# Convolutional attention on one core: first image's query norms taken with chunk-wise products, and 36 convolution taps of its second row group moved to TensorE

## The chip, the cores and the metric

The kernel runs on one core of one Trainium2 chip. The metric is the device time of one execution in microseconds (us). Before the change the median of three runs is 2868.29 us (2864.83 to 2871.43). The execution that was profiled took 2862.87 us, of which the trace spans 2861.1 us; the remaining 1.8 us lie outside the program's first and last instruction.

## What is computed

The input is four images of 384 channels and 48 x 48 points, in 32-bit floats. The reference, cut to what matters here:

```
local = depthwise 7x7 convolution of x, scaled and shifted per channel
x_norm = layernorm(x over channels)
q, k, v = split(x_norm @ qkv_w.T + qkv_b), 8 heads of 48
q = q + layernorm(local over channels)
attn = softmax(q @ k.T / sqrt(48)); out = attn @ v
out = x + (out @ proj_w.T + proj_b)
```

So every query needs the convolution of its point and a layernorm of it over the 384 channels ("the query norm"), on top of the usual projection.

## The kernel before

Channels lie on the partitions, in three chunks of 128. An image's 2304 points are cut into six groups of 8 image rows, 384 points each; there are 24 groups in all, counted by `t`. Keys and values of a whole image are made first (`from_x`, L574), then the six query groups are run one after the other. A group's attention is 12 slots (`for s in range(NSLOT)`, L1111): four pairs of heads, and three batches of six key blocks for each. A slot has two halves. In the first, TensorE (PE) makes the scores (`score_batch`, L888) and ScalarE (ACT) exponentiates them (L896); in the second, PE weighs the values (`weigh_batch`, L903).

The convolution runs beside that on VectorE (DVE), as one multiply-add for each of 49 taps and three chunks (L288, or L284 for a first tap): 147 operations for a group. All groups' operations stand in one stream, in order (`conv_ops`, L263; `stream`, L929). `convolve(point)` takes the number of operations that `plan` (L362) has given to a half slot. The plan knows for each half slot a spare DVE time (`spare`, L315) and for each group a due point: `due` (L359) asks that the 147 operations of group t are through before half 0 of slot `norm_slots(t - 1)[0]` of the group before. That slot is 8 in group 0 and 5 in all later ones (L313). The plan takes at each half slot the fastest rate that any of the next twelve due points asks for, so an early due point makes all that comes before it denser.

When a group's convolution is done, its query norm follows (class `Norm`, L384), spread over slots:

- For group 1, worked on in group 0 (slots 7 to 11): DVE adds the three chunks (`sum`, L408 and L409), PE multiplies the sum by a matrix of 1/384 (`mean_kept`, L429) to have the mean on every partition, ACT copies it to SBUF (L431), DVE subtracts it (`centre`, L440), ACT squares (L403), and the same sum and product of the squares give the variance. ACT takes its root (`root`, L447 to L449), DVE refines it (`newton`, L454 and L455).
- For all other groups: DVE adds the chunks, transposes in blocks of 32 and reduces (L464, L465), two DMAs on SP's queue write the partial sums to DRAM and read them back spread over the partitions (`out`, L468 and L469), and DVE reduces those (`few_in`, L478), transposes back (L485, L505) and goes on. That happens twice for a norm, for the mean and for the variance; the root is taken of 12 numbers a partition (L497 to L499).

Then `local_end` (L738) scales the convolution, `query_end` (L747) adds it to the projected query, `high_queries` (L760) and `low_queries` (L765, with the `qs<-qs` DMAs of L770 and L772 on SP) split the query of a head pair in two parts and place them for the scores, and `gather_tails` (L521) collects the fourth pair.

The order of the instructions on PE, DVE and ACT is the order of the program's text (L84); each of them works through its own list in order. SP's and POOL's lists are ordered by the framework. PSUM is four buffers of two banks, taken in turn by everything on PE.

At the start of the kernel (L948 to L1037) keys, values and projected queries of the first image are made, with the norms of x on PE and the convolution of group 0 and the first 10 operations of group 1 on DVE (`convolve_first`). Ten taps of chunk 0 of group 0 are done on PE as products with a diagonal matrix of the tap's 128 weights (`first_products`, L298). ACT makes those matrices (L296). The stage ends with `query_end(0)`, `high_queries(0, 0)`, `low_queries(0, 0)` (L1031 to L1033), and the scores of group 0 begin.

Of the kernel before, what the change touches and what calls it, by code (L numbers as in the profile page):

```python
# [16 lines left out]
P = 128  # L17
# [11 lines left out]
OUT_SLOT = 4  # L29
WARM = 14  # L30
PE_TAPS = 10

# [13 lines left out]
def unshifted_pass(  # L46
# [39 lines left out]
    def two_banks(name="r"):  # L86
        return ps.tile([P, 2, 512], F32, tag="r", name=name)
# [175 lines left out]
    def conv_ops(t):  # L263
        b, g = divmod(t, NG)
        if t + 1 < NT:
            load_slab(*divmod(t + 1, NG))
        slab, first, end = slabs[b, g]
        acc = work.tile([P, CC, G], F32, tag="acc", name=f"acc{t}", bufs=3)
        accs[t] = acc
        if t == 0:  # L270
            nc.vector.memset(acc[:, 0, :], 0.0)

        order = [(tap, c) for tap in taps for c in range(CC)]
        if t == 0:
            mine = [(tap, 0) for tap in taps[PE_TAPS:]]
            order = [o for o in order if o[1]] + mine
        for tap, c in order:
            part = window(slab, acc[:, c, :], g, first, end, c, tap)
            if not part:
                continue  # L280
            src, dst = part
            weight = cw[:, c, tap : tap + 1]
            if tap == taps[0]:
                nc.vector.tensor_scalar(  # L284
                    dst, src, weight, shift[:, c : c + 1], ALU.mult, ALU.add
                )
            else:
                nc.vector.scalar_tensor_tensor(dst, src, weight, dst, ALU.mult, ALU.add)  # L288
# [9 lines left out]
    def first_products():  # L298
        first_sum = two_banks()[:, 0, :G]
        slab, first, end = slabs[0, 0]  # L300
        for i, tap in enumerate(taps[:PE_TAPS]):
            src, part = window(slab, first_sum, 0, first, end, 0, tap)
            nc.tensor.matmul(
                part, lhsT=diagonal(i), rhs=src, start=i == 0, stop=i == PE_TAPS - 1
            )
        return first_sum
# [77 lines left out]
    class Norm:  # L384
# [38 lines left out]
            self.m = two_banks()[:, 0, :G] if m is None else m  # L423
            project(self.m, lambda c: mean_w, lambda c: src[:, c, :])

        def mean_kept(self):

            m = two_banks()[:, 0, :G]
            nc.tensor.matmul(m, lhsT=mean_w, rhs=self.buf[:, 0, :], start=True, stop=True)  # L429
            self.m = self.buf[:, 0, :]  # L430
            nc.scalar.copy(self.m, m)  # L431

# [540 lines left out]
    next(making)  # L973
    for c in range(CC):
        scale_rows(0, c)
    first_sum = first_products()
    m, bank = columns()
    convolve_first(10)
    norm = Norm(xn[0, 1])
# [15 lines left out]
    norm.scale(norm.newton())  # L995
    both(making)
    convolve_first(7)
    for g in range(1, NG):

        last = g == NG - 1  # L1000
        making = from_x(0, g)
        both(making)
        assert not last or n_first >= each - PE_TAPS
        norm = Norm(accs[0] if last else xn[0, g + 1])
        norm.mean_by_chunk(norm.src)
        if last:
# [24 lines left out]
    query_end(0)  # L1031
    high_queries(0, 0)
    low_queries(0, 0)  # L1033
# [5 lines left out]
    for t in range(NT):  # L1039
        b, g = divmod(t, NG)  # L1040
        if g == 0 and b:
# [4 lines left out]
            for gk in range(NG):  # L1046
# [57 lines left out]
                both(making)  # L1104
                if gk < NG - 2:
                    ao = fetch(before + 1)
        following = g < NG - 1
        next_image = b + 1 < B
        coming = next_image and g >= later(b + 1)
        first, second = norm_slots(t)  # L1110
        for s in range(NSLOT):  # L1111
            pair, third = divmod(s, KB // BATCH)
            if third == 1 and pair < NP - 1:
                high_queries(t, pair + 1)
            score_batch(t, s)
            if pair < NP - 1 or g < NG - 1:
                load_keys(b, (pair + 1) % NP, third)
# [17 lines left out]
            if coming and s == X_SLOTS[1] + 1:  # L1135
                norm_x.scale(norm_x.few_newton())
            if following and s == second + 1:
                local_end(t + 1, norm.few_newton() if t else norm.newton())
# [8 lines left out]
            if t and following and s == second:  # L1147
                norm.few_variance()
            convolve("slot", t, s, 0)
            sums_add()  # L1150
            if t == 0 and s in (first, second):
                norm.mean_kept()
            if coming and s == X_SLOTS[1]:
                norm_x.few_root()
            if following and s == second:
                norm.few_root() if t else norm.root()
            if s == first and t == 0:
                norm.centre()
# [9 lines left out]
            if t and following and s == first:  # L1168
                norm.few_centre()
            if s == OUT_SLOT and g:  # L1170
                ao = outputs[t - 1][0]
# [9 lines left out]
            if following and s == first - 1:  # L1181
                norm = Norm(accs[t + 1])
                norm.sum()
                if t:
                    norm.out()
            if following and s == first + 1:
                norm.sum_squares()
                if t:
                    norm.out()

    sums_add()
    for before in range(NT - NG, NT):
# [556 lines left out]
```

## Time and profile before

| what | value |
|---|---|
| median of three runs | 2868.29 us |
| profiled execution | 2862.87 us, span 2861.1 us |
| PE, DVE, ACT busy | 2771.2, 2458.6, 1635.9 us |
| start to the first score of group 0 | 164.4 us |
| group 0, 1, 2, 3, 4, 5 (first score to first score) | 116.1, 101.8, 104.8, 104.0, 101.0, 88.4 us |
| keys and values of image 1 | 139.9 us |
| groups 6 to 10 (image 1) | 90.4, 88.3, 91.6, 98.2, 90.1 us |

A group's time is the distance between the first score product of its slot 0 and that of the next group; it is read off the timeline. A slot without a wait takes 7.36 us, so a group takes at least 12 x 7.36 = 88.3 us. The profile's windows view gives for each stretch of time the busy microseconds of every engine and the number of its instructions, and then the granted share of TensorE's clock. A product of 32-bit floats shows as two matmul records.

### The profile page before, as it was taken

What the parts mean: (1) busy time and instruction counts of PE and PEld (TensorE: products, weight loads), DVE (VectorE), ACT (ScalarE), POOL (GpSimd) and SP (SyncE); (2) the same over time, 40 slices, a digit from 0 to 9 for tenths busy, and PEclk for the clock granted to TensorE, in tenths of its full rate; (3) what the DMA queues carried; (4) which work ended last, traced back from release to release, by engine and by line L of the source; (5) the groups of instructions that cost most, each with busy time, mean ns of one, the idle gap of its engine ahead of it and who ended that gap; (6) DMA issues with size and microseconds to landing.
All of it is one profiled execution on the core that took longest, in us unless ns stands there. A gap on an engine that the chain in (4) does not pass through costs nothing.

```text
span 2861.1 us, 53602 instructions
## 1 busy us (share of the span) xinstructions
PE 2771.2 (97%) x19238; PEld 1742.0 (61%) x19238; DVE 2458.6 (86%) x4875; ACT 1635.9 (57%) x2632; POOL 592.4 (21%) x1125
## 2 busy tenths in 40 slices
PE   9987989899999999999999999999999999999999
PEld 6654555565655666656665666666665566666665
DVE  7789898899889999988989999989988999999502
ACT  4345656566622766666642466766662266676662
POOL 5720000000067001000026401000005610011000
PEclk9998999999999999999999999999999999999999
DMA  7444444544555555446445554554554555445541
GB/s 140 107 138 113 130 123 133 149 127 129 145 153 136 170 155 164 126 136 179 150 112 155 167 148 148 170 154 128 150 157 136 140 169 159 139 136 179 168 160 62
DMA packets 197461, 410.57 MB, mean 144 GB/s; under 512 B 69888, under 2 KB 140480, under 8 KB 196672
## 3 DMA queue, kind: packets, MB, share of 16 engines
q0 software_dynamic: 65440, 254.88, 26.9%
q1 hardware_dynamic: 128752, 148.55, 21.2%
q8 instruction: 154, 2.52, 0.4%
q10 hardware_dynamic: 2992, 3.62, 0.4%
q14 instruction: 123, 1.01, 0.1%
HBM read 298.44 MB, written 64.78 MB: 127 GB/s over the span
## 4 chain that ended last, share of the span: by engine, by line
PE 69%; DVE 18%; DMA 8%; POOL 2%; issue 1%; ACT 1%; SPq 1%; DVEq 0%; ACTq 0%; POOLq 0%
PE o L903 30%; PE r L888 26%; PE r L515 13%; DVE acc L288 13%; DMA parts<-part 2%; DMA four<-parts 2%; DMA wide<-k 1%; DMA qs<-qs 1%; DMA slab<-in_x_dram 1%; POOL wide L540 0%; DVE ao L807 0%; DVE sq L409 0%; DVE qs L765 0%; DMA start_up<-in_qkv_wT_dram 0%; DVE k L603 0%
## 5 line engine op out<-in xcount | busy, mean ns | idle before, releaser
L288 DVE SCALAR_TENSOR_TENSOR acc<-slab,vec,acc 128x368 f32<-128x368 f32 (+6 forms) x3447 | 1767.7, 581 | 1.2
L896 ACT ACTIVATE pt<-r 128x768 f32<-128x768 f32 x1728 | 1250.1, 829 | 154.1 <-PE r L888 113.5
L903 PE MATMUL o<-pt,v 128*64 128x384 f32 x6912 | 1182.2, 492 | 0.0
L888 PE MATMUL r<-qs,ks 64*128 64x384 f32 x10368 | 1020.8, 345 | 73.2 <-DMA qs<-qs 38.9
L888 PEld LDWEIGHTS r<-qs,ks 64*128 64x128 f32 x10368 | 908.8, 188 | 264.5 <-issue 203.2
L903 PEld LDWEIGHTS o<-pt,v 128*64 128x64 f32 x6912 | 472.1, 137 | 591.7 <-issue 516.7
L572 POOL DMA_DIRECT2D ks<-wide x276 | 199.3, 724 | 1831.2 <-PE r L888 1800.0
L788 ACT COPY o<-o 113x384 f32<-113x384 f32 x192 | 92.0, 479 | 381.0 <-PE o L903 378.6
L515 PE MATMUL r<-xn,w_qk 128*128 128x384 f32 x864 | 283.7, 486 | 0.0
L515 PEld LDWEIGHTS r<-xn,w_qk 128*128 128x128 f32 x864 | 164.3, 190 | 114.4
L515 PE MATMUL r<-w_v,xn 128*128 128x384 f32 x432 | 145.1, 488 | 0.8 <-ACT w_v L701 0.8
L592 ACT COPY v<-r 128x384 f32<-128x384 f32 x72 | 32.1, 480 | 194.6 <-PE r L515 194.6
L478 DVE TENSOR_REDUCE few<-four 128x12 f32<-128x48 f32 x80 | 18.5, 231 | 124.9 <-DMA four<-parts 124.7
L807 DVE TENSOR_TENSOR ao<-ao,o 113x384 f32<-113x384 f32 x144 | 79.3, 551 | 48.2 <-ACT o L788 48.1
L515 PE MATMUL r<-af,w_o 128*128 128x384 f32 x360 | 119.1, 487 | 0.0
L515 PEld LDWEIGHTS r<-w_v,xn 128*128 128x128 f32 x432 | 81.6, 190 | 59.3 <-issue 2.4
L798 ACT COPY ao<-o 113x384 f32<-113x384 f32 x72 | 34.4, 478 | 127.9 <-PE o L903 127.9
L515 PEld LDWEIGHTS r<-af,w_o 128*128 128x128 f32 x360 | 68.3, 190 | 47.8 <-issue 0.6
L540 POOL DMA_DIRECT2D wide<-k x192 | 96.2, 505 | 4.2 <-issue 2.6
L562 POOL DMA_DIRECT2D wide<-k x192 | 93.2, 491 | 8.8 <-DMA wide<-k 6.0
L556 POOL DMA_DIRECT2D wide<-k x144 | 70.7, 494 | 97.6 <-ACT k L600 69.0
L617 ACT ACTIVATE xn<-r,qkb 128x384 f32<-128x384 f32 x72 | 40.2, 577 | 58.6 <-PE r L515 57.3
(129 smaller groups left out, 1159.5 us busy)
## 6 DMA issues: line engine op xcount, KB each, us to landing
ks<-wide POOLq DMA_DIRECT2D x276, 768.0 KB, 6.9
qs<-qs SPq DMA_DIRECT2D x528, 48.0 KB
xr<-in_x_dram SPq DMA_DIRECT2D x24, 576.0 KB
slab<-in_x_dram SPq DMA_DIRECT2D x32, 378.0 KB
wide<-k POOLq DMA_DIRECT2D x480, 24.0 KB, 2.1
held<-ao SPq DMA_DIRECT2D x20, 576.0 KB
af<-held SPq DMA_DIRECT2D x20, 576.0 KB
rb<-rden SPq DMA_DIRECT2D x48, 216.0 KB
```

The lines of the kernel that those rows point to most:

```text
L288: nc.vector.scalar_tensor_tensor(dst, src, weight, dst, ALU.mult, ALU.add)
L515: nc.tensor.matmul(dst, lhsT=weights(c), rhs=src(c), start=c == 0, stop=c == CC - 1)
L540: queue.dma_start(out=dst[r + 32 * i : r + 32 * i + 32, 1], in_=k[r + 16 : r + HD, 1])
L556: nc.gpsimd.dma_start(out=last[16 * u : 16 * u + 16, 0], in_=k[r : r + 16, 0])
L562: nc.gpsimd.dma_start(out=last[to : to + 16, 1], in_=k[r : r + 16, 1])
L572: nc.gpsimd.dma_start(out=stacks[b, p].bitcast(F32)[:, :, at], in_=wide[b, p][:, :, at])
L617: nc.scalar.activation(src[:, i, :], q[:, :G], AF.Identity, bias=qkb[:, 0, i : i + 1])
L788: nc.scalar.copy(part[0 : 64 + HA], sums[0 : 64 + HA, 0, :G])
L807: nc.vector.tensor_add(dst, dst, part[0 : 64 + HA])
L888: nc.tensor.matmul(r[:, j, :G], lhsT=ks[rows, w, kb * P : (kb + 1) * P], rhs=qs[rows, m, :], start=i == 0, stop=i == 2,)
L896: nc.scalar.activation(pt, r[:, :, :G], AF.Exp, scale=SCALE)
L903: nc.tensor.matmul(sums[halves[j], 0, :G], lhsT=values[t // NG, kb // NB][:, first : first + 64], rhs=pt[:, j, :], start=i == 0, stop=i == ...
```

## The change

1. Groups 1 to 5 (those whose query norm is worked on inside the first image, `t + 1 < NG`) all use PE for the norm, without the DVE sums: `mean_kept(src)` multiplies the three chunks by the 1/384 matrix and accumulates, three products instead of one and two DVE additions. `out`, `few_in` and what belongs to them go for groups 2 to 5.
2. The stages of that norm sit elsewhere: mean products after the weighing of slot `first`, centring in half 0 of slot `first + 1`, products of the squares and the root after the weighing of `first + 1`, refining, `local_end` and `query_end` in half 0 of `first + 2`, `high_queries`, `low_queries` and the gathering at `first + 3`. `first` is 8 in group 0 and 7 in groups 1 to 4.
3. The due points of groups 1 to 5 move with it, to half 1 of `first`, and the table of spare times is another there.
4. 36 of the 49 taps of chunk 0 of group 1 are taken out of the DVE stream and done as PE products at the end of the start stage; ACT makes the 36 diagonal matrices, nine at the head of each of four rounds of the key and value loop, and writes the sum with the shift into the accumulator.

```diff
+MORE_TAPS = 36
...
-        if t == 0:
-            mine = [(tap, 0) for tap in taps[PE_TAPS:]]
+        if t < 2:
+            mine = [(tap, 0) for tap in taps[(PE_TAPS, MORE_TAPS)[t] :]]
             order = [o for o in order if o[1]] + mine
...
+    def products(g, n, diagonal):
+        total = two_banks()[:, 0, :G]
+        slab, first, end = slabs[0, g]
+        for i, tap in enumerate(taps[:n]):
+            src, part = window(slab, total, g, first, end, 0, tap)
+            nc.tensor.matmul(part, lhsT=diagonal(i), rhs=src, start=i == 0, stop=i == n - 1)
+        return total
+
+    more = []
+
+    def more_diagonal(i):
+        return more[i // 9][:, i % 9 * P : i % 9 * P + P]
+
+    def make_more():
+        for tag, bufs in (("qs", 5), ("qs", 5), ("ao", 2), ("rb", 1)):
+            d = work.tile([P, CC, G], F32, tag=tag, name="more", bufs=bufs)
+            more.append(d.rearrange("p c g -> p (c g)"))
+            for i in range(9 * len(more) - 9, 9 * len(more)):
+                nc.scalar.mul(more_diagonal(i), ident, cw[:, 0, taps[i] : taps[i] + 1])
+            yield
...
     def norm_slots(t):
-        return (5, 8) if t else (8, 10)
+        return (8 - (t > 0), None) if t + 1 < NG else (5, 8)
...
-        if t == 0:
-            time -= {(7, 1): 1.1, (8, 1): 1.4, (9, 1): 1.1, (11, 0): 5.0}.get((s, half), 0.0)
+        if t + 1 < NG:
+            time -= {(first + 1, 0): 1.4, (first + 2, 0): 4.3, (first + 3, 0): 0.6}.get(
+                (s, half), 0.0
+            )
...
-        last = ("slot", t - 1, norm_slots(t - 1)[0], 0) if t % NG else ("kv", t, 4, 0)
-        due.append((points.index(last), t * each))
+        last = ("slot", t - 1, norm_slots(t - 1)[0], t < NG) if t % NG else ("kv", t, 4, 0)
+        due.append((points.index(last), t * each - MORE_TAPS))
...
-        def mean_kept(self):
+        def mean_kept(self, src):
             m = two_banks()[:, 0, :G]
-            nc.tensor.matmul(m, lhsT=mean_w, rhs=self.buf[:, 0, :], start=True, stop=True)
+            project(m, lambda c: mean_w, lambda c: src[:, c, :])
...
+    making_more = make_more()
     for g in range(1, NG):
         last = g == NG - 1
+        next(making_more, None)
         making = from_x(0, g)
...
+    nc.scalar.activation(
+        accs[1][:, 0, :], products(1, MORE_TAPS, more_diagonal), AF.Identity, bias=shift[:, 0:1]
+    )
     query_end(0)
     high_queries(0, 0)
     low_queries(0, 0)
...
-        following = g < NG - 1
+        early = t + 1 < NG
+        following = g < NG - 1 and not early
...
+            if early and s == first + 3:
+                high_queries(t + 1, 0)
             score_batch(t, s)
...
+            if early and s == first + 3:
+                low_queries(t + 1, 0)
+                gather_tails(*reversed(queries[t + 1]))
             convolve("slot", t, s, 0)
             sums_add()
-            if t == 0 and s in (first, second):
-                norm.mean_kept()
+            if early and s == first + 1:
+                norm.centre()
+                jobs.extend(norm.square_jobs())
+            if early and s == first + 2:
+                local_end(t + 1, norm.newton())
+                query_end(t + 1)
...
             weigh_batch(t, s)
+            if early and s == first:
+                norm = Norm(accs[t + 1])
+                norm.mean_kept(norm.src)
+            if early and s == first + 1:
+                norm.mean_kept(norm.buf)
+                norm.root()
...
```

More of the change, by code (lines that the diff above doesn't have):

```diff
@@ L296, in make_diagonals @@
             nc.scalar.mul(diagonal(i), ident, cw[:, 0, taps[i] : taps[i] + 1])
[L298 to L306, printed above, removed]
+    def products(g, n, diagonal):
[15 more added lines that the diff above has]
+            yield
     def norm_slots(t):
-        return (5, 8) if t else (8, 10)
+        return (8 - (t > 0), None) if t + 1 < NG else (5, 8)
     def spare(t, s, half):
@@ L975, in unshifted_pass @@
         scale_rows(0, c)
-    first_sum = first_products()
+    first_sum = products(0, PE_TAPS, diagonal)
     m, bank = columns()
@@ L1137, in unshifted_pass @@
             if following and s == second + 1:
-                local_end(t + 1, norm.few_newton() if t else norm.newton())
+                local_end(t + 1, norm.few_newton())
                 query_end(t + 1)
@@ L1146, in unshifted_pass @@
                 norm_x.few_variance()
-            if t and following and s == second:
+            if following and s == second:
                 norm.few_variance()
+            if early and s == first + 3:
+                low_queries(t + 1, 0)
+                gather_tails(*reversed(queries[t + 1]))
             convolve("slot", t, s, 0)
             sums_add()
-            if t == 0 and s in (first, second):
-                norm.mean_kept()
+            if early and s == first + 1:
[4 more added lines that the diff above has]
+                query_end(t + 1)
             if coming and s == X_SLOTS[1]:
@@ L1155, in unshifted_pass @@
             if following and s == second:
-                norm.few_root() if t else norm.root()
-            if s == first and t == 0:
-                norm.centre()
+                norm.few_root()
             weigh_batch(t, s)
+            if early and s == first:
[4 more added lines that the diff above has]
+                norm.root()
             if third == 1 and pair < NP - 1:
@@ L1167, in unshifted_pass @@
                 norm_x.few_centre()
-            if t and following and s == first:
+            if following and s == first:
                 norm.few_centre()
@@ L1183, in unshifted_pass @@
                 norm.sum()
-                if t:
-                    norm.out()
+                norm.out()
             if following and s == first + 1:
                 norm.sum_squares()
-                if t:
-                    norm.out()
+                norm.out()
     sums_add()
```

## The prediction

> **What bounds the kernel now.** I read the windows view first, cut at the first score of each group, to see which engine fills each stretch (after the length: PE, PEld, DVE, ACT, POOL busy with instruction counts, then clock, DMA share, GB/s).
>
> ```profile
> 34.00:150.00 116.00, 116.00 (x373) 69.28 (x373) 91.44 (x166) 40.44 (x71) 81.75 (x166) 1.00 0.45 108
> 150.00:164.40 14.40, 6.18 (x20) 3.32 (x18) 10.66 (x20) 3.19 (x6) 8.49 (x17) 0.83 0.71 239
> 164.40:280.50 116.10, 96.20 (x725) 60.13 (x725) 113.04 (x219) 63.26 (x96) 15.24 (x25) 0.91 0.41 119
> 280.50:382.30 101.80, 94.76 (x722) 60.81 (x722) 94.05 (x185) 61.12 (x93) 8.65 (x12) 0.94 0.41 120
> 382.30:487.10 104.80, 94.67 (x724) 60.20 (x722) 94.41 (x186) 61.40 (x94) 8.65 (x12) 0.93 0.44 131
> ...
> 692.10:780.50 88.40, 88.40 (x723) 56.80 (x722) 81.71 (x170) 60.38 (x94) 5.13 (x16) 1.00 0.53 151
> 780.50:920.40 139.90, 139.41 (x432) 81.88 (x432) 126.71 (x245) 35.98 (x76) 88.00 (x180) 1.00 0.50 137
> ```
>
> The start stage (34 to 150) is PE's: 116.00 of 116.00 us. Group 5 (692 on) is PE's too, at 88.40 us. But group 0 takes 116.10 us, of which DVE works 113.04; in groups 1 to 4 DVE works 88 to 94 us of 101 to 105. The waits of DVE from 164.4 to 780 us say what it does in the rest:
>
> ```profile
> DVE few L478 <- DMA four<-parts: 41.7, 7, 10.6
> DVE qs L765 <- ACT qs L760: 2.8, 1, 2.8
> DVE sq L408 <- ACT sq L403: 1.2, 1, 1.2
> ```
>
> So in groups 0 to 4 DVE is either busy or waits for the norm's trip through DRAM: for group 2, 94.4 + 9.8 (its part of the first line) = 104.2 of 104.8 us. DVE sets the end there, and the chain of waits agrees: from 176 to 617 us it runs through runs of L288, then `parts` and `four` transfers. The five groups lie 527.7 - 5 x 88.4 = 85.7 us above what PE alone needs.
>
> The third view is the timeline at the seam between start stage and scores:
>
> ```profile
> 146.35 9.84 PE L515 MATMUL r<-xn,w_qk 128*128 128x384 f32 x30
> ...
> 156.70 0.50 ACT L760 CAST qs<-xn 128x384 fp32r<-128x384 f32 x1
> ...
> 157.23 0.56 DVE L765 TENSOR_TENSOR qs<-xn,qs 128x384 fp32r<-128x384 f32 x1 [3.67 <-ACT qs L760]
> ...
> 158.83 13.54 DVE L288 SCALAR_TENSOR_TENSOR acc<-slab,vec,acc 128x368 f32<-128x368 f32 x26
> ...
> 164.44 0.66 PE L888 MATMUL r<-qs,ks 64*128 64x384 f32 x1 [8.25 <-issue]
> ```
>
> PE is free from 156.2 to 164.4 us while ACT's and DVE's split of the queries and its DMAs run.
>
> **What the Trainium skill says.** "TensorE: Matmul & The Clock Gate", section "Architectural detail: the array is 16× 32×32, not 1× 128×128": ACT and DVE queues are strictly first in, first out. The trace agrees: nothing passes L478 in the up to 10.6 us that it waits. The same page, "What's actually happening": after an idle window of about 3.4 us PE's clock is halved. The trace agrees: the granted clock is 0.91 to 0.95 in groups 0 to 4, which have idle PE time, and 1.00 in group 5. "DMA: Bandwidth & Descriptors", section "Anatomy of one DMA — SWDGE (gpsimd) path", puts a fixed cost of about 2 us on a DMA; these two hops (on SP's queue, so another path) cost DVE up to 10.6 us at once, so the trace's figure is used.
>
> **The change part by part.** All sums are against the profiled 2862.9 us (span 2861.1 and 1.8 around it).
>
> *36 taps on PE: +22 us on the path.* L303's 10 taps are 20 records in 6.12 us, 0.306 us a record; full L515 records come every 116.4 / 372 = 0.313 us. 72 records with windows of 360 to 384 columns (mean 371) cost 72 x 0.313 x 371/384 = 21.8 us. They stand in PE's order after its last product of the stage, so they run from 156.2 to 178.0. ACT's write of the sum (0.59 us as L600) waits for them, and behind it on ACT is `high_queries(0, 0)`, so L760 goes from 156.7 to about 178.9: +22.2. Behind it in turn wait DVE's L765, the two key operations L603 with POOL's `wide` writes, the `qs` DMAs on SP, and the first scores: 164.4 becomes 186.6. The gap of 8 us on PE is not used up by the products; it comes again after them, as the ACT-DVE-DMA chain follows. SP's queue is emptier then (three of its gathering DMAs now go ahead), worth 0 to 1.5 us; I take 0. DVE stands still for 22 us, but the 26 operations that it did in the old gap find the same 7 us before the scores, so its head start stays. POOL's late `wide` writes have until slot 2's load, 15 us later: nothing.
> *The 36 matrices:* 36 at 0.29 us (L296: ten in 2.6 us plus the last) are 10.4 us of ACT, in four bursts of 2.6 us. A burst comes after the query copies of a round, where ACT then waits 3.3 us for PE (ahead of L592). Hidden: 0; uncovered, at most 10.
>
> *DVE in groups 0 to 4.* An L288 takes 77.1 / 147 = 0.52 us of DVE. I worked the plan through with the old and the new tables. Planned operations in groups 0 to 5 were 202, 167, 148, 149, 126, 130; they become 154, 150, 150, 150, 131, 134. That is 53 fewer: 36 are on PE, 17 go to image 1. Group 0: 197 were in its window, so 43 x 0.52 = 22.4 us go, and the four additions (2.2): 113.0 becomes 88.4. Group 2 (likewise 1 and 3): additions 2.2, four transposes 2.3, two L465 1.1, the small ones 1.1 go, L454 and L455 (1.2) come: 94.4 becomes about 89. Group 4 likewise about 89. The trips through DRAM go, 41.7 us less what image 1's x norm still needs in groups 4 and 5 (3.3 in group 5, about the same in 4): some 35 us of stall. In their place DVE waits for the root: in step with PE it reaches L454 some 5 us early, because PE's slot is longer by the products. So DVE needs about 89 plus 0 to 5; the wait shrinks as DVE falls behind.
>
> *PE in groups 0 to 4.* Six products, 12 records at 0.313: +3.75 us a group, so 88.4 becomes 92.1. New too is that the copy and the root (0.47 + 0.62 + 0.52 + 0.52, as L431 and L447 to L449 in group 0) stand on ACT ahead of the next slot's exponentials, whereas before they had the weighing's 4 us to hide behind. No row shows this place: between 0 (the exponentials take 4.3 of a slot's 7.36 us) and 2.4 us; below 0 is excluded, since it only adds. With four PSUM buffers PE gets some scores ahead; I take 1.3. So 93.4 for PE against 89 to 94 for DVE: what is late next is PE itself.
> Sum: group 0, 93.4 + 3.4 (its slot 0 was 10.75 instead of 7.36 us, at half clock after the gap, which stays) = 96.8; groups 1 to 3, 93.5 each; group 4, 95 with the x norm's trip. 472.3 against 527.7: -55.4.
>
> *Image 1.* 17 more operations, 8.9 us of DVE, mostly in stages that PE fills (139.41 of 139.90 us). Groups 8 and 9 (91.6, 98.2 us) have DVE and SP waits of their own, and get two and four more. Between -5 and +8; I take +3.
>
> 22.2 - 55.4 + 3 = -30.2: 2832.7 as profiled. The median of the runs lies 5.4 above the profiled one, so I predict 2868.3 - 30.2 = 2838.1.
>
> **The rivals.**
> *A, as above* (2838). For it: group 7, with DVE busy 84.6 us, ran in 88.3 without a wait, so a nearly full DVE need not hold PE.
> *B, the chain of the norm takes the place of the DRAM trip.* PE, ACT and DVE now hand over five times in three slots (mean, centre, squares, root, `newton`), and PE itself stands in the chain. With about 4 to 5 us lost in each group beyond A, the groups come to about 98: -30.2 + 22 = -8, 2860. For it: DVE's 89 us and 5 us of root wait leave little. Against: the wait shrinks with its lag.
> *C, slower: PE held by DVE at the mean products.* Group 0 had such a product:
>
> ```profile
> PE r L429 <- DVE sq L409: 7.4, 1, 7.4
> ```
>
> With the half clock after it slot 8 took 18.28 us (first scores at 228.72 and 247.00) instead of 7.36 + 0.6, a loss of 10.3. Now every group has one. It decides where DVE enters slot `first` later than the 3.5 us between its half and PE's turn. In all five groups: 5 x 10.3 - 5 x 1.3 = +45, so 2883. Against: that lag came from 19 operations a slot (9.9 us) in group 0; now it is 14 (7.3).
> *D, cheaper seams:* no ACT loss (-6.5), image 1 gains (-3 - 2): 2827.
>
> **How the numbers follow.** A 0.64, B 0.18, C 0.08, D 0.10. A alone is 2828 to 2848 (the root 0 to 2.4 us a group, image 1 -5 to +8, the seam). The range 2826 to 2858 holds A, nearly all of D and the nearer part of B; C and the rest lie outside. 0.2%, 5.7 us, is about what a measurement can tell from no change. Faster by more: A, D and two thirds of B, 0.86; within: 0.06; slower: C, 0.08.
>
> **What would show it.** First score of group 0 at 186 to 187; 72 product records, about 22 us, before it. Groups 1 to 4 at 93 to 95, with PE busy nearly all of it at clock 1.00. No wait at L478 before group 4; DVE waits of up to 5 us at `newton`. Wrong would be: a long PE wait on DVE at the mean products (C), groups of 98 with waits on the root, or scores waiting for `qs` (B), v copies late in the start stage, or image 1 longer by over 8 us.

## The result, and the profile after

| | before | after |
|---|---|---|
| median of 20 runs each | 2867.43 us (2856.68 to 2877.45) | 2863.93 us (2856.2 to 2871.85) |
| ratio after / before | | 0.9987 [0.9977, 0.9998] |
| profiled execution | 2862.87 us | 2871.85 us, span 2870.1 |

The change is worth 3.5 us, 0.13%, which is no change by the measure of 0.2%. The prediction was 2838.1 us with a range of 2826 to 2858; the measured median lies above that range.

The profiled execution of after happens to be the slowest of its 20 runs (8 us above its median), and that of before lies 5 us below its own. The two profiles therefore differ by +9 us where the medians differ by -3.5. A sum over stages is only useful as far as the programs differ, so I cut both traces at the first score of each group and list what each stretch took.

| stretch, us | before | after | predicted for after |
|---|---|---|---|
| start to first score of group 0 | 164.4 | 182.3 | 186.6 |
| group 0 | 116.1 | 97.2 | 96.8 |
| group 1 | 101.8 | 101.3 | 93.5 |
| groups 2, 3 | 104.8, 104.0 | 93.7, 93.7 | 93.5, 93.5 |
| group 4 | 101.0 | 93.7 | 95 |
| group 5 | 88.4 | 88.4 | 88.4 |
| end of image 0 | 780.5 | 750.5 | 747.3 |
| keys and values of image 1 | 139.9 | 140.3 | |
| groups 6, 7, 8, 9, 10 | 90.4, 88.3, 91.6, 98.2, 90.1 | 91.8, 95.8, 103.2, 98.2, 96.3 | |
| sum of groups 6 to 10 | 458.6 | 485.3 | about 461.6 (+3 for image 1) |

Image 0 gains 30.0 us, close to the 33.2 predicted. The first five groups of image 1 give 26.7 back. At the end of group 10 after is 3.0 us ahead, close to the 3.5 of the medians. The later groups have the same plan in both kernels; in these two profiles after loses 12 us there, which I take for the spread of single runs.

The windows view of after shows both halves of this (after the length: PE, PEld, DVE, ACT, POOL busy with instruction counts, clock, DMA share, GB/s). The rows are the seam, groups 0, 1 and 2 of image 0, and groups 7 and 8 of image 1.

```profile
150.00:182.30 32.30, 28.22 (x90) 16.65 (x89) 6.09 (x12) 3.77 (x7) 6.20 (x13) 0.99 0.28 101
182.30:279.60 97.30, 95.83 (x733) 60.91 (x733) 88.06 (x168) 62.67 (x95) 17.51 (x30) 0.97 0.43 125
279.60:380.90 101.30, 96.28 (x735) 61.11 (x734) 90.24 (x174) 63.16 (x96) 8.65 (x12) 0.97 0.47 138
380.90:474.60 93.70, 92.95 (x734) 58.68 (x732) 89.92 (x174) 62.61 (x96) 8.64 (x12) 1.00 0.51 145
...
982.50:1078.30 95.80, 90.65 (x723) 57.68 (x721) 82.98 (x164) 60.80 (x94) 8.65 (x12) 0.96 0.49 145
1078.30:1181.50 103.20, 94.52 (x724) 61.56 (x722) 87.17 (x172) 61.76 (x94) 8.64 (x12) 0.93 0.43 133
```

Group 2 is now PE's: 92.95 of 93.70 us at clock 1.00, with DVE at 89.92 beside it. It was DVE's before. But groups 7 and 8 of image 1 are nobody's. In group 8 DVE works 87.17 of 103.20 us, PE 94.52 at a clock of 0.93: PE idles, and then runs slower. In before the same two groups looked like this, group 7 being full:

```profile
1010.90:1099.10 88.20, 88.20 (x722) 56.61 (x720) 84.68 (x166) 60.70 (x94) 8.64 (x12) 1.00 0.50 155
1099.10:1190.70 91.60, 89.67 (x723) 56.38 (x722) 80.73 (x159) 60.83 (x94) 8.64 (x12) 1.00 0.50 150
```

The work of DVE doesn't explain it: in group 7 DVE works *less* in after (82.98 us against 84.68) and the group is 7.6 us longer. The waits do. First the waits of DVE in groups 7 to 10 of after (total, times, longest), then those of before:

```profile
DVE few L492 <- DMA four<-parts: 35.6, 6, 10.5
DVE rd L841 <- DMA rd<-den: 12.9, 2, 9.1
```

```profile
DVE few L478 <- DMA four<-parts: 24.1, 6, 7.6
DVE rd L827 <- DMA rd<-den: 2.7, 1, 2.7
```

The trip through DRAM that the change takes out of image 0 is still there in image 1, and it costs DVE 11.5 us more than before; the softmax's denominators (`rd<-den`), which are read back from DRAM too, cost it another 10.2. PE's waits in the same stretch show how it is reached: in after 15.4 us on ACT's `ao` copy (L812) against 1.4 in before.

**One such trip in both kernels.** A trip has two hops: the write of the partial sums (`parts<-part`) and their reading back (`four<-parts`). This is group 7 in after, around its first trip. "SPq" and "POOL" rows are DMA issues, and in brackets stands the idle time before an instruction with what ended it:

```profile
1023.03 0.72 POOL L586 DMA_DIRECT2D ks<-wide  x1 [19.91 <-PE r L902]
1023.39 0.55 DVE L479 TENSOR_REDUCE part<-sq 128x12 f32<-128x384 f32 x1
1023.97 0.59 SPq L482 DMA_DIRECT2D parts<-part  x1
...
1030.39 0.58 SPq L483 DMA_DIRECT2D four<-parts  x1
1036.98 0.23 DVE L492 TENSOR_REDUCE few<-four 128x12 f32<-128x48 f32 x1 [8.49 <-DMA four<-parts]
...
1040.51 0.46 ACT L812 COPY ao<-o 113x384 f32<-113x384 f32 x1
1041.03 1.33 PE L902 MATMUL r<-qs,ks 64*128 64x384 f32 x6 [5.15 <-ACT ao L812]
```

And the same trip in before:

```profile
1045.64 0.55 DVE L465 TENSOR_REDUCE part<-sq 128x12 f32<-128x384 f32 x1
1046.22 0.59 SPq L468 DMA_DIRECT2D parts<-part  x1
1048.77 0.58 SPq L469 DMA_DIRECT2D four<-parts  x1
1051.30 0.22 DVE L478 TENSOR_REDUCE few<-four 128x12 f32<-128x48 f32 x1
1051.36 0.72 POOL L572 DMA_DIRECT2D ks<-wide  x1 [19.91 <-PE r L888]
```

In before the write is issued at 1046.22 and the partial sums are back at 1051.30, 5.1 us, in the time that DVE has convolutions to do; the three key loads `ks<-wide` (768 KB each) start afterwards, at 1051.36. In after the reduction comes 6 us later in the group, behind the first key load (1023.03). Each hop takes 6.4 to 6.6 us instead of 2.5, together 13.0, and DVE stands for 8.49 us. Behind the reduction L492 on DVE stands the centring (L500), behind that ACT's squares (L417), behind them on ACT the copy L812, and behind that PE, idle for 5.15 us and then at a lower clock (0.71 from 1041 to 1048 us).

Key loads come in threes, 3.7 us into slots 2, 5, 8 and 11, released by a head pair's last scores. The reduction belongs to slot 4. As long as DVE is on time the trip passes ahead of slot 5's loads; some microseconds of lateness put it among them. The Trainium skill, "DMA: Bandwidth & Descriptors", section "Queues, rings and completion order", points the same way: a DMA engine changes between the queues it has work for, a whole packet at a time. Between 1023 and 1037 us of after the DMA view gives 432 packets with 2.36 MB in POOL's queue (50.9% of the engines' time) and 934 with 1.29 MB in SP's (38.5%): the key loads' packets are 5.5 KB each on average, those of SP's queue, which also carries `held<-ao` and loads of x, 1.4 KB, so a small transfer that takes turns with them would wait long for its turns. That this is how the time is lost fits these numbers, but no run here separates it from a mere lack of bandwidth.

**Group 8, the largest loss.** Its first trip is not the reason: DVE waited 7.6 us for it in before and waits 6.3 in after. But DVE comes late into the group, and so the reading of group 7's denominators meets the key loads of slot 2. After:

```profile
1096.71 2.16 POOL L586 DMA_DIRECT2D ks<-wide  x3 [19.89 <-PE r L902]
1098.82 0.77 SPq L840 DMA_DIRECT2D rd<-den  x1
1104.91 5.30 PE L902 MATMUL r<-qs,ks 64*128 64x384 f32 x31 [3.55 <-DMA qs<-qs]
1106.30 0.30 DVE L841 RECIPROCAL rd<-rd 128x24 f32<-128x24 f32 x1 [9.11 <-DMA rd<-den]
```

And before:

```profile
1113.79 0.35 SPq L826 DMA_DIRECT2D rd<-den  x1
1115.53 0.30 DVE L827 RECIPROCAL rd<-rd 128x24 f32<-128x24 f32 x1 [2.71 <-DMA rd<-den]
1117.56 2.16 POOL L572 DMA_DIRECT2D ks<-wide  x3 [19.91 <-PE r L888]
```

Issued ahead of the loads, the reading took 1.7 us; behind them it took 7.5. The query transfers (`qs<-qs`) that were under way beside the same loads held PE for 3.55 us, and slot 3 took 13.8 us instead of 7.36.

**Why DVE is late in image 1.** Image 0 has 53 planned convolution operations fewer; 36 of them are on PE, and 17 have gone into image 1 because the later due points ask for less in image 0. The stretch of keys and values got 124 instead of 121, groups 6 to 10 got 136, 134, 133, 122, 118 instead of 133, 130, 131, 118, 117.

### The profile page after: what moved, and what is told of

It is laid out like the page before. It is cut to its first block, busy times and chain, and to the rows that moved or that the text cites. A ratio compares the mean times of both kernels' runs of the same rounds, so it can differ in the third digit from the quotient of the medians.

```text
span 2870.1 us, 53777 instructions
## 1 busy us (share of the span) xinstructions
PE 2802.3 (98%) x19366; PEld 1757.3 (61%) x19366; DVE 2419.7 (84%) x4783; ACT 1653.8 (58%) x2677; POOL 592.4 (21%) x1125
## 4 chain that ended last, share of the span: by engine, by line
PE 72%; DVE 15%; DMA 8%; ACT 1%; issue 1%; POOL 1%; SPq 1%; ACTq 0%; DVEq 0%
PE o L917 30%; PE r L902 25%; PE r L529 16%; DVE acc L289 9%; DMA four<-parts 2%; DMA qs<-qs 1%; DMA parts<-part 1%; PE r L304 1%; DVE sq L478 1%; DMA wide<-k 0%; DVE sq L423 0%; ACT pt L910 0%; DVE part L479 0%; DVE sq L422 0%; DMA slab<-in_x_dram 0%
## 5 line engine op out<-in xcount | busy, mean ns | idle before, releaser
L289 DVE SCALAR_TENSOR_TENSOR acc<-slab,vec,acc 128x368 f32<-128x368 f32 (+4 forms) x3412 | 1751.6, 585 | 1.6
L902 PE MATMUL r<-qs,ks 64*128 64x384 f32 x10368 | 1010.6, 343 | 56.1 <-ACT ao L812 26.0
L492 DVE TENSOR_REDUCE few<-four 128x12 f32<-128x48 f32 x72 | 16.7, 232 | 117.1 <-DMA four<-parts 117.1
L812 ACT COPY ao<-o 113x384 f32<-113x384 f32 x72 | 34.4, 478 | 131.9 <-PE o L917 131.9
L554 POOL DMA_DIRECT2D wide<-k x192 | 96.5, 507 | 2.9 <-issue 2.6
L576 POOL DMA_DIRECT2D wide<-k x192 | 92.8, 489 | 11.4 <-DMA wide<-k 9.6
L779 DVE TENSOR_TENSOR qs<-xn,qs 128x384 fp32r<-128x384 f32 x72 | 39.9, 554 | 55.9 <-ACT qs L774 55.8
```

The source lines that it names most:

```text
L554: queue.dma_start(out=dst[r + 32 * i : r + 32 * i + 32, 1], in_=k[r + 16 : r + HD, 1])
L576: nc.gpsimd.dma_start(out=last[to : to + 16, 1], in_=k[r : r + 16, 1])
L779: nc.vector.tensor_sub(qs[:, 1, :], query_of(t, p), qs[:, 0, :])
L902: nc.tensor.matmul(r[:, j, :G], lhsT=ks[rows, w, kb * P : (kb + 1) * P], rhs=qs[rows, m, :], start=i == 0, stop=i == 2,)
```

## The experiments

My theory, called L in the expectations: the 17 operations make DVE some microseconds later in image 1, and that lateness puts the trips behind the key loads. The rivals are that the loss in image 1 comes of something else in the change, or that one part of the change is worth nothing by itself. Ratios are against before on the same chip, with 95% intervals.

### Give image 1 its old load: e1_pull_back

```diff
         due.append((points.index(last), t * each - MORE_TAPS))
+    due.insert(NG - 1, (points.index(("kv", NG, 0, 0)), 896))
```

> The changed kernel with one more due point: 896 operations of the stream through at the end of image 0, which gives image 1 exactly the plan that it had before the change (kv stage 121, groups 6 to 10 132, 131, 131, 118, 117 operations); the 17 operations come back to groups 0 to 5 (156, 151, 151, 151, 135, 142). Theory L (lateness: the 17 operations moved into image 1 make DVE late there, so that its trips through DRAM meet the burst of key loads at 3.7 us into slot 5, and each costs PE 6 to 8 us): groups 7 to 10 fall from 393.5 us to about 370 (before the change 368.2), the end of image 0 stays within 5 us of 750.5, the whole 15 to 25 us under the changed kernel, 2840 to 2850. Theory J (chance: those trips are long or short from run to run whatever the plan): groups 7 to 10 stay at 385 to 395, the whole at 2860 or above.

Measured: 2839.83 us, ratio 0.9925 [0.9907, 0.9943], where after has 0.9987. One more due point, which changes only when DVE does the operations, brings 0.62%, some 18 us (25 in groups 6 to 10 of the two profiles). Groups 6 to 10 took 90.5, 88.3, 94.3, 97.4, 89.8, together 460.3 instead of 485.3. In groups 7 to 10 DVE's wait for the denominators (L841 in after) fell from 12.9 to 4.2 us. Group 7 in the windows view of e1:

```profile
981.90:1070.20 88.30, 88.30 (x724) 56.69 (x722) 85.92 (x168) 60.73 (x94) 8.64 (x12) 1.00 0.54 157
```

In group 7 DVE works 85.92 us, 2.9 more than in after, and PE has no gap. The due point costs image 0 no more than about a microsecond (groups 0 to 4: 97.8, 102.0, 93.7, 93.7, 93.8).

### Give before the new load: e2_push_before

```diff
         room += [spare(t, s, h) for s in range(NSLOT) for h in range(2)]
+    for i, point in enumerate(points):
+        if point[:2] == ("slot", NG - 1):
+            room[i] *= 0.83
```

The factor 0.83 on group 5's spare times moves 17 operations into image 1, as the change does.

> The kernel before, with the spare times of group 5 cut to 0.83, so that 17 operations move from image 0 into image 1 (end of image 0 at 915 operations instead of 932), as the change does; nothing else. Theory L: groups 7 to 10 rise from 368.2 us towards 390, the whole by 10 to 25 us, 2877 to 2892. Theory J: within 5 us of the kernel before.

Measured: 2889.59 us, ratio 1.0095 [1.0076, 1.0114]: +27 us, without any part of the change. Groups 6 to 10: 93.4, 95.9, 101.7, 96.9, 96.5, together 484.4, almost those of after (485.3). Group 7 in the windows view of e2, to be laid beside its 88.20 us in before and 95.80 in after:

```profile
1012.20:1108.10 95.90, 91.18 (x724) 58.05 (x722) 83.32 (x164) 60.97 (x94) 8.65 (x12) 0.96 0.49 145
```

e1 and e2 together show that the loss in image 1 is one of the load, in both directions, and not of the new norm or the products.

### The norm alone: e3_norm_only

```diff
-MORE_TAPS = 36
+MORE_TAPS = 0
...
-        next(making_more, None)
...
-    nc.scalar.activation(
-        accs[1][:, 0, :], products(1, MORE_TAPS, more_diagonal), AF.Identity, bias=shift[:, 0:1]
-    )
```

> The changed kernel without the 36 taps on PE (all operations of group 1 on DVE again), with the norm by products and the later due points kept. The products cost 18 us at the seam (first score 164.4 became 182.3) and took 25 planned operations, 13 us, out of group 0 and 7 out of group 1. Both theories: first score at 164 to 165, group 0 at 103 to 108 us instead of 97.2, group 1 at 95 to 103, end of image 0 at 740 to 752. Theory L: image 1 as bad as in the changed kernel (same plan there), whole 2855 to 2866. If the taps were what pays: above 2866.

Measured: 2849.58 us, ratio 0.9957 [0.9942, 0.9973], so it is faster than the whole change by 0.3% and below the 2855 to 2866 that I expected. Image 0 ended at 743.9 us (after: 750.5), with the first score back at 164.5 and group 0 at 108.7. In group 0 the prediction's rival C appears, in slot 8, which took 20.9 us (waits of PE in e3):

```profile
PE r L529 <- DVE acc L289: 9.4, 1, 9.4
```

PE stands at the mean products and waits for the last convolution operation of DVE. With the 36 operations still on DVE group 0 is too full. In groups 2 to 4 (93.8, 93.7, 93.7) nothing is lost. Groups 6 to 10 took 480.1, which is the loss of image 1 again.

### No key loads in the way: e4_no_burst

```diff
     def load_keys(b, p, i):
+        if b == 1 and p >= 2:
+            stacks[b, p] = stacks[b, p - 2]
+            return
```

In image 1 this kernel leaves out the key loads of head pairs 2 and 3, which are those issued in slots 2 and 5.

> The changed kernel, but in image 1 the keys of pairs 2 and 3 are not loaded (their scores use the keys of pairs 0 and 1, so image 1's output is not the reference's): the two bursts of three key loads of 786 KB in slots 2 and 5 of groups 6 to 10 are gone, DVE's plan is untouched. Theory L, with the burst as what makes a late trip long: trips of groups 7, 8 and 10 that took 11 to 14 us take 5 to 8, DVE waits at the reduction of them under 3 us each, groups 7 to 10 fall from 393.5 to about 365 to 375, whole 2838 to 2850. If SP's order or the trip itself is what is long: trips and groups as in the changed kernel, within 5 us of it.

Measured: 2826.39 us, ratio 0.9877 [0.9859, 0.9895], below the 2838 to 2850 expected. Groups 6 to 10: 91.6, 88.3, 91.2, 90.6, 88.9, together 450.6, which is 8 us less than in before too. DVE is as late as in after, but its trip in group 7 passes (timeline of e4):

```profile
1024.00 0.59 SPq L482 DMA_DIRECT2D parts<-part  x1
1026.72 0.58 SPq L483 DMA_DIRECT2D four<-parts  x1
1029.09 0.24 DVE L492 TENSOR_REDUCE few<-four 128x12 f32<-128x48 f32 x1 [0.57 <-DMA four<-parts]
```

It takes 5.1 us from the write's issue, at the same place in the group (slot 5, 4.2 us) at which after takes 13.0. The table has the first trip of the query norm in each group: where its reduction began, then how long after the reduction's end the sums were back, and how much of that DVE waited:

| query norm's first trip in | before | after | e4 |
|---|---|---|---|
| group 7 | slot 4, 5.4 us: 5.1 / 0 | slot 5, 4.1: 13.0 / 8.5 | slot 5, 4.2: 5.1 / 0.6 |
| group 8 | slot 5, 0.8: 12.6 / 7.6 | slot 5, 6.4: 11.4 / 6.3 | slot 5, 7.0: 5.5 / 0.5 |
| group 9 | slot 6, 0.3: 7.7 / 4.2 | slot 5, 6.4: 11.8 / 8.3 | slot 5, 6.1: 4.6 / 1.0 |
| group 10 | slot 5, 0.7: 5.7 / 2.5 | slot 5, 2.2: 13.7 / 10.5 | slot 5, 1.9: 6.5 / 3.3 |

The table also shows that the loads were costing before something in groups 8 and 9. One limit: the edit takes away slot 2's loads too and lowers the whole traffic (99 to 104 GB/s in groups 7 to 10 instead of 133 to 145), so it shows that the key loads do it, not that slot 5's alone do.

The trips' lengths go with the order of issue rather than with the slot; no experiment moved that order alone. In before the reductions of groups 8 and 10 begin within 0.1 us of the same place, but group 10's read-back leaves 0.1 us ahead of the first key load (1329.40 and 1329.52 us) and the trip takes 5.7 us; group 8's leaves 0.8 us behind it (1140.42 and 1139.64) and the trip takes 12.6. The same holds for the trips of groups 6 to 10 in all eleven traces with every key load, counted from the write's issue and only where DVE waited 0.3 us or more. Of 29 whose read-back left before any load, with none in the 9 us before the write either, 28 took 4.2 to 5.9 us and one 8.2. Of 20 with a load issued less than 4.5 us before the write or between the two hops, all took 8.5 to 14.1 us. Between, 5 to 9 us after the loads, 21 trips took 4.2 to 10.8 us.

### The products alone: e5_taps_only

Before, with the 36 taps of group 1's chunk 0 as products (the `products`, `more_diagonal` and `make_more` of the change) and the due points 36 lower.

> The kernel before with the 36 taps on PE alone (norms and due points as before, each due 36 operations lower, so image 1 has the plan of before). The seam costs 18 us as in the changed kernel (first score at 182), groups 0 and 1 are planned 25 and 11 operations fewer at 0.515 us, 18.5 us. If groups 0 and 1, which DVE sets, give back just what DVE sheds: end of image 0 within 4 us of 780.5, whole within 6 us of the kernel before. If the taps are a gain of their own: under 2855. If the seam is not paid back: over 2875.

Measured: 2878.04 us, ratio 1.005 [1.0032, 1.0068]: slower by 16 us. That is the expectation's case "over 2875", but not its reason, since the seam was mostly paid back. The first score came at 182.8. Groups 0 to 4 took 107.6, 97.7, 105.4, 103.7, 98.0, and image 0 ended at 783.6 instead of 780.5. So 18 us were paid at the seam and 15 came back in groups 0 to 4. In group 0 of e5 DVE still sets the end: it works 105.84 of 107.50 us. The profile explains 3 us in image 0 and 4 in groups 6 to 10 (462.5); the rest lies in later groups, whose plan is unchanged, and stays open.

### The chain first, then the products: e6_chain_first

Built on e1:

```diff
-    nc.scalar.activation(
-        accs[1][:, 0, :], products(1, MORE_TAPS, more_diagonal), AF.Identity, bias=shift[:, 0:1]
-    )
     query_end(0)
     high_queries(0, 0)
     low_queries(0, 0)
+    nc.scalar.activation(
+        accs[1][:, 0, :], products(1, MORE_TAPS, more_diagonal), AF.Identity, bias=shift[:, 0:1]
+    )
```

> The kernel of e1 with the query chain of group 0 (query_end, high_queries, low_queries) ahead of ACT's write of the 36 taps' sum, so that ACT and DVE don't wait for PE's products and the chain runs under them. The first score comes straight after the products, at 178 instead of 182.1, slot 0 of group 0 takes 7.4 to 8 us instead of 11.5 (no idle PE, no half clock), DVE starts its operations 20 us earlier. Expected whole: e1 less 6 to 8 us, 2832 to 2834. If the 22 us in which DVE stood still cost more than the seam shows: below 2828. If the DMAs of the queries were what the scores waited for: within 3 us of e1, 2839.

Measured: 2825.32 us, ratio 0.9867 [0.9843, 0.9891], 14.5 us below e1. First the seam as the change has it (timeline of after):

```profile
155.61 22.61 PE L304 MATMUL r<-slab,more 128*128 128x384 f32 x72
178.26 0.58 ACT L1047 ACTIVATE acc<-r,vec 128x384 f32<-128x384 f32 x1 [21.86 <-PE r L304]
178.74 0.50 ACT L774 CAST qs<-xn 128x384 fp32r<-128x384 f32 x1
182.33 0.66 PE L902 MATMUL r<-qs,ks 64*128 64x384 f32 x1 [4.11 <-issue]
```

ACT waits 21.86 us for the products; behind that wait stands its cast, and behind the cast DVE. In e6 the cast is issued ahead of that wait:

```profile
155.75 22.61 PE L304 MATMUL r<-slab,more 128*128 128x384 f32 x72
156.44 0.50 ACT L775 CAST qs<-xn 128x384 fp32r<-128x384 f32 x1
158.56 10.95 DVE L289 SCALAR_TENSOR_TENSOR acc<-slab,vec,acc 128x360 f32<-128x360 f32 x21
178.29 3.44 PE L903 MATMUL r<-qs,ks 64*128 64x384 f32 x36
```

The queries' chain runs beside the products, DVE convolves in the meantime, and the scores begin as the last product ends. Slot 0, which takes 10.9 us in after, with a clock of 0.50 over its first 3.7 us, takes 7.4 at clock 1.00. By the start of image 1's first group that is 8.6 us in the profile; I had expected 6 to 8 for the whole. The medians differ by 14.5; the rest lies later and is not explained.

### The norm with image 1's old load: e7_norm_pulled

e3 with the due point of e1, at 932 (the 36 operations are on DVE again).

> The kernel of e3 (norm by products, no taps on PE) with a due point of 932 operations at the end of image 0, so that image 1 has the plan of before. Theory L: groups 7 to 10 from 388 us to about 370, the whole 15 to 22 us under e3's 2849.6, 2828 to 2835, and below e1 (2839.8), the same kernel with the taps. Theory J: within 5 us of e3.

Measured: 2831.57 us, ratio 0.9888 [0.9867, 0.9909], 18 us below e3; groups 6 to 10 took 462.0 instead of 480.1, also 18. The same edit is worth the same with and without the products. And the products, as the change places them, cost: e1's median is 8 us above e7's.

### The norm one slot earlier in group 0: e8_slot_seven

Built on e6. It came from a wait left over in group 1, slot 0 (timeline of after), which holds 7.6 us that the prediction did not have:

```diff
-        return (8 - (t > 0), None) if t + 1 < NG else (5, 8)
+        return (7, None) if t + 1 < NG else (5, 8)
```

```profile
275.91 2.16 POOL L586 DMA_DIRECT2D ks<-wide  x3 [25.36 <-PE r L902]
276.86 1.32 SPq L786 DMA_DIRECT2D qs<-qs  x2
284.89 1.61 PE L902 MATMUL r<-qs,ks 64*128 64x384 f32 x7 [2.63 <-DMA qs<-qs]
```

The norm that is worked on in group 0 ends with `high_queries` in slot 11, where three key loads are issued among the DMAs of group 1's queries.

> The kernel of e6 with the norm of group 1 in slot 7 as that of the others (8 before). In the changed kernel slot 0 of group 1 took 14.9 us: the query transfers of slot 11 leave at the same time as the burst of key loads at 3.7 us into slot 11 and land after 7.6 us of PE waiting. In slot 10 they are ahead of it. Expected: slot 0 of group 1 at 7.4 to 8 us, whole 7 us under e6. If it is only that the chain is one slot too short, the same; if DVE is then late at the mean product of slot 7, PE waits there and the gain is under 3 us.

Measured: 2816.98 us (2810.3 to 2831.84), ratio 0.9844 [0.9817, 0.9871]. In e8 the DMAs go out in slot 10, before the loads, and group 1 starts without a gap (93.7 us):

```profile
262.29 1.22 SPq L787 DMA_DIRECT2D qs<-qs  x2
268.66 2.17 POOL L587 DMA_DIRECT2D ks<-wide  x3 [23.21 <-PE r L903]
```

Groups 0 to 4 are 93.8, 93.7, 93.7, 93.7, 93.8. This is the lowest median of the study, 1.6% below before, though its interval overlaps with that of e6; groups 6 to 10 (462.1) are about as in before. That the same key loads held up the queries fits the order of issue, but e8 also gives the chain one slot more, so it does not separate the two.

### More work ahead: e9_more_ahead, e10_most_ahead

In e8 DVE works 79.0 of group 0's 93.80 us. So I tried to fill the rest and relieve image 1 further (e10: 1.4 and 940):

```diff
+    room[: 2 * NSLOT] = [time * 1.3 for time in room[: 2 * NSLOT]]
...
-    due.insert(NG - 1, (points.index(("kv", NG, 0, 0)), 896))
+    due.insert(NG - 1, (points.index(("kv", NG, 0, 0)), 930))
```

> The kernel of e8 with the spare times of group 0 raised by 1.3 and the due point at the end of image 0 at 930 operations instead of 896: group 0 gets 200 operations instead of 156 (DVE is busy only 79 of its 94 us there and comes with 20 us of head start), groups 1 to 5 two fewer each, image 1's kv stage 116 instead of 121 and its groups 6 to 10 129, 126, 126, 115, 114 instead of 132, 131, 131, 118, 117. Theory L: the first sums of group 8, 1.6 us into slot 5 in e8, come before slot 5, its trip falls from 13 to about 5 us, group 8 from 93.7 to 88 to 90, group 9 or 10 may gain too: whole 5 to 12 us under e8 (2817). If what is left in groups 8 to 10 is not lateness: within 4 us of e8. If group 0 can't take 44 more: its slots from 7 on grow past 9.5 us and the whole rises.

> As e9 with factor 1.4 and 940 operations: group 0 214, groups 1 to 5 148, 148, 149, 132, 139, kv stage 116, groups 6 to 10 127, 126, 125, 114, 113. Theory L: as e9 or 1 to 4 us below it, since the lateness of group 8 is then gone already; group 0's DVE needs about 109 us of the 94 and its 20 of head start, so PE begins to wait at slot 7 or at slot 0 of group 1 if this is too much.

Measured: 2830.67 us, ratio 0.9905 [0.9886, 0.9924], and 2838.05, ratio 0.9932 [0.9914, 0.9949]: both slower than e8. Image 1 did mostly as L says (e10: groups 7 to 10 at 88.3, 88.3, 88.2, 92.9; e9's group 8 at 88.3, but its group 10 at 94.7 instead of e8's 90.9). But groups 0 and 1 went up to 103.4 and 102.5 in e9, and 108.2 and 103.0 in e10. Slot 8 of group 0 took 19.2 us in e9, with the first of these lines among PE's waits; the second is from e10, groups 0 and 1:

```profile
PE r L531 <- ACT sq L419: 8.0, 1, 8.0
```

```profile
PE r L904 <- DMA qs<-qs: 12.8, 5, 5.4
```

In e9 DVE centres too late, so ACT squares too late, so PE stands at the products of the squares. In e10 that wait is only 2.5 us. There PE waits mostly for query transfers: a late DVE puts those of slot 5 of group 0 beside that slot's key loads (issued from 218.55 us on, the loads at 219.29), and slot 6 takes 17.6 us. Group 1 has such a wait in both kernels, 5.6 us in e9. So DVE's free time in group 0 can't be filled that densely: PE depends on DVE at the norm and at the queries.

## Why the prediction was wrong

**Right: groups 0, 2, 3 and 4.** With the steps "DVE in groups 0 to 4" and "PE in groups 0 to 4" these groups came out within 1.3 us each: PE's 93.7 against 88 to 90 for DVE. Only DVE's work in group 4 was off, 84.3 us where "about 89" stood, without effect, since PE is the later one. Slots without a product take 7.36 us, the two with mean products 9.49, which is 2.1 more (1.9 was the price of six records), and the slot with the root's hand-over 8.55, 1.2 more, where I took 1.3 between 0 and 2.4. DVE's wait for the root was up to 5.7 us per group, against "some 5". The DRAM trip is down to 0.8 us of waiting in all of image 0. Rival B didn't come. Rival C didn't come either, but e3 shows that it is near: 9.4 us at the mean products where group 0 keeps its 36 operations. In e9 a wait of the same kind, 8.0 us, stands at the products of the squares.

**Right in kind, a little off: the seam.** The products cost 22.61 us (predicted 21.8), and the first score moved by 17.9 instead of 22.2. The 36 matrices cost nothing: the products begin at 155.6. The term that was too small is the SP queue's relief, "worth 0 to 1.5 us; I take 0": after the products the chain needed 4.1 us to the first score, where before it needed 8.25. The first four query DMAs left SP's queue within 2.4 us (179.26 to 181.67), in before within 5.4 (157.23 to 162.60), which is 3.0 of the 4.1 us gained. That left the prediction 4.3 us too high there.

**Missing: group 1's slot 0.** I put nothing on the queries of group 1. They are still split in slot 11 of group 0, as in before, beside that slot's key loads, and before's slot 0 of group 1 had taken 10.5 us instead of 7.36. It cost 7.6 us (101.3 against 93.7 for its neighbours), and e8 removed it. These two errors almost cancel by luck: 30.0 us measured for image 0, 33.2 predicted.

**Wrong: "Image 1."** This is the step that failed. It read: "17 more operations, 8.9 us of DVE, mostly in stages that PE fills [...] Between -5 and +8; I take +3." It was +27. The count of operations was right, and so was the 8.9 us: from 750.5 to 1376.0 us of after DVE works 558.1 us, in the same stages of before 549.2. What failed is the price: I took the lateness of DVE as a shift of at most its own length, covered by PE. I had seen that groups 8 and 9 "have DVE and SP waits of their own", and did not ask what those waits depend on. They depend on how the small transfers fall to the key loads. A trip ahead of them takes some 5 us, one among them 8.5 to 14, and in after it is followed by a wait of DVE of 6 to 10 us, an idle PE and a slower clock. DVE's lateness carries over from group to group. In before the first trip of the query norm was slowed in groups 8 and 9 only; in after it is slowed in every group from 7 to 10, and in group 8 the queries and the denominators meet slot 2's loads as well. e1 takes the 17 operations back and wins 18 us (0.62%), e2 moves them without the change and loses 27, e4 keeps the lateness and takes the loads away and wins 1.1%, some 32, more than the change had lost: three readings of one cause. With +27 in the place of +3 the prediction's own sum would have been 2862.

The prediction's list of what would make it wrong ends in "image 1 longer by over 8 us". That was the place, and its range still allowed no more than 8 there.

**What the change's parts are worth.** The norm by products is worth 12.6 us as it stands (e3) and 30 with the old load in image 1 (e7). The 36 products lose time where the change puts them (e5, and e1 against e7), and no longer lose it once the queries' chain goes ahead of them: e6 lies 6 us below e7, which has no products, but their intervals overlap.

**Open.** Runs of one kernel spread by 8 us or more to either side, and groups with the same plan in both kernels do too (group 16 took 89.3 us in before's profile and 96.3 in after's). There too it goes with the order of issue: a trip of that group was written 3.1 us ahead of the first key load in before and took 6.3 us, 1.8 us ahead in after and took 15.1. What moves DVE by that one microsecond from run to run stays open. Open are also whether e8 gains by the order of the transfers or by the one slot more, the remainder of e5, the later part of e6's gain, and whether the transfers are slowed by the packets of the other queue or by bandwidth.

## What to carry to other kernels

Moving a due point moves the work somewhere else: find out where, and price it there by what waits for its engine and by which transfers that waiting step then meets, not by its own duration. A small transfer on the critical chain is cheap or dear depending on what large transfer stands beside it, so a lateness can cost several times its length: here 8.9 us of DVE cost 27. And in in-order queues place a dependency chain ahead of the long filler: the same 36 products cost 14 us less, 9 of them seen in the profile, when the queries' split stood in front of them.

## What the runs showed of the hardware

- A write of 6 KB to DRAM and the reading back of 24 KB took 5.1 us (group 7 in before), and 11 to 14 us (groups 7 to 10 in after) while three loads of 768 KB were under way from another queue; in group 7 each hop went from 2.5 to 6.5 us. A read-back issued 0.1 us ahead of the first load was not slowed (5.7 us in all), one issued 0.8 us behind it was (12.6). The Trainium skill, "DMA: Bandwidth & Descriptors", section "Latency and other measured facts", names memory latency as the main part of a DMA's fixed cost of about 2 us, and says that it grows with the load on the memory; the direction agrees, the size here is larger.
- A short stretch of full traffic did not do that: in before the DMA engines moved 354 to 440 GB/s from 1046.3 to 1047.6 us, in the first hop of the trip shown above, all of it from SP's own queue, and that hop still took 2.55 us.
- 72 records of fp32 products came every 0.314 us and ran back to back with the scores that follow in e6 at full clock, while after the 4 us gap in after the clock was 0.50 for 3.7 us, 0.72 over the slot, which took 10.9 us instead of 7.36.
